# Weight transform spread over the first part and six node batches of a graph-layer kernel

## The chip, the cores and the metric

The kernel runs on one core of a Trainium2 chip. The metric is the device time of one execution in microseconds (us), lower is better. A run has several executions on the same chip as executions of the kernel before.

Names in the profile: PE is TensorE, DVE is VectorE, ACT is ScalarE, POOL is GpSimd, SP is SyncE; SPq and ACTq are the queues in which SyncE and ScalarE issue transfers. PEclk is the clock that the throttle granted to TensorE, 1.00 being full speed. TensorE's tiles: pw is a piece of the weight transform, phT, pc and px are the transpose, conv1 and the windows of the first part; ps, pm, pd, pa and pn are s, the messages, the distances, adj and A times the messages in a node batch, and py is a frequency product.

## The reference, cut to what matters

```python
h = jnp.maximum(_layernorm(x), 0.0)                    # x: 32 batches, 512 x 256, f32
xc = transpose(h)
c = relu(bn1(conv1d(xc, conv1_w, 0)))                  # conv1: 1 tap
c = bn2(conv1d(c, conv2_w, 8))                         # conv2: 17 taps
x_conv = transpose(relu(c + xc))
s = h @ w_se.T + b_se
A = exp(-distance(s)) * adj                            # 512 x 512 a batch
x_nmp = A @ relu(h @ w_msg.T + b_msg)
return x + GRU(concat(x_conv, x_nmp), h)
```

The kernel computes conv2 in a frequency domain. For that the 17-tap weights are transformed once, in 16 pieces ("the weight transform"), and written to a DRAM tensor WD. The 32 batches go in two groups of 16. For group 0 the order is: first part (layer norm, transpose, conv1, windows to frequency), then node batches (A, the messages, x_nmp), then the same first part for group 1, then the rest. Forty frequency products a group use the transformed weights, and each product needs all 16 pieces.

## The kernel before

```python
def load_taps(gen, pc):                                 # 8 transfers
    t = W2P[pc] = gen.tile([P, PI, D], FP, tag="w2p", bufs=2)
    for q in range(4):
        # ... two nc.sync.dma_start into rows of t ...

def weights_to_freq(gen, pc, part):                     # one piece
    for q in range(4):
        WST[q] = gen.tile([ROWS, SI, D], FP, tag="wst", bufs=6)     # staging
    # ... 8 matmuls pw, each into a PSUM bank ...
            for q in range(4):
                if q % 2:
                    nc.vector.tensor_copy(dst, src)     # eviction to staging
                else:
                    nc.scalar.copy(dst, src)
    for q in range(4):
        nc.sync.dma_start(WD[:, i0 : i0 + SI, :], WST[q])

def load_x(b):
    X[b] = work.tile([P, NC, D], FP, tag="x", bufs=2)
    nc.sync.dma_start(X[b], x[b].rearrange("(c p) d -> p c d", p=P))

# layer_norm(b):   statistics on VectorE, rstd on GpSimd, normalising on VectorE
# transpose_h(b):  phT on TensorE, hT = relu(phT) on VectorE, hT to DRAM (HD) on SyncE's queue
# conv1(b):        pc on TensorE, h = pc + shift on VectorE, relu on ScalarE
# windows_to_freq: px on TensorE, xf on ScalarE

def first_part(g, xf, between):
    # ...
    for b in range(b0, b1):
        if b + 1 < b1:
            layer_norm(b + 1)
        if b + 2 < b1:
            load_x(b + 2)
        between(b - b0)
        conv1(b)
        if b + 1 < b1:
            transpose_h(b + 1)
        windows_to_freq(b, xf)

with phase("first", "gen"):
    load_taps(gen, 0); load_taps(gen, 1)
    early = 12
    def between(i):
        for pc, part in spread(pieces, i, early) if i < early else []:
            weights_to_freq(gen, pc, part)
            if part == PI // SI - 1 and pc + 2 < QI // PI:
                load_taps(gen, pc + 2)
        # ...
    first_part(0, xf, between)
with phase("pw"):
    with phase("nodes"):
        # load_nodes, embed, message of batch 0
        for b in range(GB):
            mine = spread(units, b, GB)                 # 40 products over 16 batches
            affinity(b); load_nodes(b + 1)              # hT and adj of the next batch
            # ... products, embed(b + 1), aggregate(b), message(b + 1), save ...
    with phase("first"):
        first_part(1, xf, lambda i: None)               # group 1
    # ...
```

A scheduler fixes the order of each engine's instructions at build time, and the transfers that an engine issues stand in that same order.

## Time and profile before

| kernel before | |
|---|---|
| median of 3 runs | 2271.43 us (2270.57 to 2273.3) |
| end of group 0's first part (last px) | 249.4 us |
| node stage of group 0 (from there to group 1's first phT) | 378.4 us |
| group 1's first part begins | 627.8 us |

I use three marks: the end of the last px of group 0, the first phT of group 1, and the difference, which I call the node stage. The next line is the table of busy times of the kernel before for that node stage. Columns: stretch, its length, then busy us of PE, weight loads, DVE, ACT and POOL with counts, then the granted clock, the DMA share and GB/s.

```profile
249.40:627.80 378.40, 378.40 (x1437) 247.28 (x1436) 104.77 (x167) 123.95 (x201) 28.28 (x39) 1.00 0.62 213
```

TensorE is busy for the whole 378.40 us at clock 1.00.

### The profile page before, as it was taken

Reading aid. Unit: us, or ns where it says so; the run is one execution under the profiler, and the core shown is the slowest. Engines: PE = TensorE matmul, PEld = TensorE weight load, DVE = VectorE, ACT = ScalarE, POOL = GpSimd, SP = SyncE. Lnnn points to the kernel's source line nnn. Section 1 sums busy time; section 2 is a strip of 40 time slices with the busy share of each in tenths; the row PEclk is TensorE's granted clock in tenths of the full one; section 3 lists DMA queues with packets and bytes.
Section 4 is the critical chain, followed back from the end, with each engine's and each line's share of the span. In section 5 each row is a group of like instructions: output and inputs, shape, how many; then the busy total and the mean of one; then the engine's idle time right before and its main releaser. Section 6 shows DMA issues by size and latency. Waiting matters only on the chain.

```text
span 2270.3 us, 20711 instructions
## 1 busy us (share of the span) xinstructions
PE 2197.3 (97%) x8000; PEld 1316.4 (58%) x8000; DVE 744.6 (33%) x1416; ACT 596.5 (26%) x946; POOL 93.0 (4%) x119
## 2 busy tenths in 40 slices
PE   5888999999999999999999999999999999999998
PEld 4556666666688555555555554555555555555554
DVE  5556422223277122321321222223322222222323
ACT  1333333333234211111111111322222322222221
POOL 1000100000011000000000000000000000000000
PEclk7888999999999999999999999999999999999999
DMA  7878665665554453464464443222222222222210
GB/s 207 275 228 264 202 235 197 221 217 198 199 190 153 119 181 118 148 194 126 129 187 132 147 143 81 71 75 64 73 64 76 78 73 64 64 64 64 64 37 19
DMA packets 207650, 308.89 MB, mean 136 GB/s; under 512 B 11713, under 2 KB 158145, under 8 KB 207553
## 3 DMA queue, kind: packets, MB, share of 16 engines
q1 hardware_dynamic: 193152, 272.93, 39.2%
q10 hardware_dynamic: 14401, 34.65, 4.1%
q8 instruction: 63, 1.03, 0.2%
q14 instruction: 34, 0.28, 0.0%
HBM read 202.68 MB, written 104.86 MB: 135 GB/s over the span
## 4 chain that ended last, share of the span: by engine, by line
PE 91%; DVE 4%; DMA 3%; issue 1%; POOL 1%; ACT 0%; SPq 0%; DVEq 0%; POOLq 0%; ACTq 0%
PE pg L411 29%; PE pgi L411 10%; PE pn L371 10%; PE py L309 9%; PE pc L401 5%; PE pd L357 5%; PE pgh L411 5%; PE pm L345 5%; PE pc L266 4%; PE pa L362 2%; PE ps L329 2%; PE px L280 2%; PE pw L216 1%; PE po L453 1%; DMA x<-in_x_dram 1%; DVE stats L235 1%
## 5 line engine op out<-in xcount | busy, mean ns | idle before, releaser
L411 PE MATMUL pg<-nmp,wih 128*128 128x512 f32 x512 | 240.8, 592 | 0.0
L411 PE MATMUL pg<-hT,whh 128*128 128x512 f32 x512 | 240.6, 592 | 0.0
L411 PE MATMUL pg<-xconv,wih 128*128 128x512 f32 x512 | 240.6, 592 | 0.0
L426 ACT ACTIVATE rz<-pg,brz 128x512 f32<-128x512 f32 x128 | 87.9, 687 | 555.3 <-PE pg L411 549.8
L371 PE MATMUL pn<-A,msg 128*128 128x512 f32 x512 | 224.9, 592 | 0.0
L363 DVE TENSOR_TENSOR A<-e,pa 128x512 f32<-128x512 f32 x128 | 86.6, 687 | 396.6 <-ACT e L359 395.6
L314 DVE COPY y<-py 128x256 f32<-128x256 f32 x78 | 33.1, 425 | 416.4 <-PE py L309 407.8
L411 PEld LDWEIGHTS pg<-xconv,wih 128*128 128x128 f32 x512 | 97.3, 190 | 122.5 <-issue 122.5
L411 PEld LDWEIGHTS pg<-nmp,wih 128*128 128x128 f32 x512 | 97.2, 190 | 122.0 <-issue 121.7
L371 PEld LDWEIGHTS pn<-A,msg 128*128 128x128 f32 x512 | 97.2, 190 | 122.0 <-issue 114.0
L411 PEld LDWEIGHTS pg<-hT,whh 128*128 128x128 f32 x512 | 97.0, 190 | 108.6 <-issue 104.3
L309 PE MATMUL py<-wt,xf 128*128 128x256 f32 x640 | 152.7, 381 | 0.0
L438 ACT ACTIVATE n<-n,vec 128x512 f32<-128x512 f32 x64 | 46.2, 722 | 329.3 <-DVE n L437 329.3
L401 PEld LDWEIGHTS pc<-back,yt 120*128 120x128 f32 x1024 | 121.9, 195 | 18.4 <-issue 18.3
L309 PEld LDWEIGHTS py<-wt,xf 128*128 128x128 f32 x640 | 121.8, 191 | 16.4
L266 PE MATMUL pc<-w,hT 128*128 128x256 f32 x512 | 130.7, 413 | 0.4 <-DVE hT L254 0.4
L357 PE MATMUL pd<-sr,sl 96*128 96x512 f32 x256 | 131.1, 593 | 0.0
L401 PE MATMUL pc<-back,yt 120*128 120x80 f32 (+1 forms) x1024 | 120.6, 277 | 3.2 <-DMA yt<-yd 3.2
L266 PEld LDWEIGHTS pc<-w,hT 128*128 128x128 f32 x512 | 105.0, 209 | 29.0 <-ACT wst L225 12.2
L411 PE MATMUL pgh<-hT,whh 128*128 128x512 f32 x256 | 120.3, 592 | 0.0
L411 PE MATMUL pgi<-nmp,wih 128*128 128x512 f32 x256 | 120.3, 592 | 0.0
L411 PE MATMUL pgi<-xconv,wih 128*128 128x512 f32 x256 | 120.3, 592 | 0.0
(78 smaller groups left out, 2364.7 us busy)
## 6 DMA issues: line engine op xcount, KB each, us to landing
wt<-wd SPq DMA_DIRECT2D x160, 384.0 KB
x<-in_x_dram SPq DMA_DIRECT2D x64, 512.0 KB
adj<-in_adj_dram SPq DMA_DIRECT2D x32, 1024.0 KB
wd<-wst SPq DMA_DIRECT2D x64, 480.0 KB
yd<-y ACTq DMA_DIRECT2D x80, 384.0 KB
yt<-yd SPq DMA_DIRECT2D x64, 480.0 KB
hT<-hd SPq DMA_DIRECT2D x48, 512.0 KB
hd<-hT SPq DMA_DIRECT2D x32, 512.0 KB
```

The source lines that it names most:

```text
L266: nc.tensor.matmul(p[:, j, :], HT[b][:, ic, c * P : (c + 1) * P], w1[:, ic, :], start=(ic == 0), stop=(ic == DC - 1))
L280: nc.tensor.matmul(p[:, j * 2 * L : (j + 1) * 2 * L], H1[b][:, c0 + j, ic * P : (ic + 1) * P], fwd, start=True, stop=True)
L309: nc.tensor.matmul(dst, v[:, ic, :], wt[:, ic, k, :], start=(ic == 0), stop=(ic == DC - 1))
L329: nc.tensor.matmul(p[:96, :], wse[:, ic, :], HT[b][:, ic, :], start=(ic == 0), stop=(ic == DC - 1))
L345: nc.tensor.matmul(p[:, j, :], HT[b][:, ic, c * P : (c + 1) * P], wmsg[:, ic, :], start=(ic == 0), stop=(ic == DC - 1))
L357: nc.tensor.matmul(pd, SL[b % 2][:, m], SR[b % 2], start=True, stop=True)
L363: nc.vector.tensor_mul(A[b][:, mc, :], e, pa)
L371: nc.tensor.matmul(p, MSG[b][:, mc, dc * P : (dc + 1) * P], A[b][:, mc, :], start=(mc == 0), stop=(mc == NC - 1))
L401: nc.tensor.matmul(p[:, t0:t1], YT[b][w][:, oc * P : (oc + 1) * P], back[:, u0 : u0 + t1 - t0], start=(w == 0), stop=(w == W - 1), skip_gr ...
L411: nc.tensor.matmul(p, w, v, start=(i == 0), stop=(i == len(terms) - 1))
L426: nc.scalar.activation(RZ[b][:, g, :], p, AF.Sigmoid, bias=brz[:, g : g + 1], scale=1.0)
L438: nc.scalar.activation(n, n, AF.Tanh, bias=b_in[:, i : i + 1], scale=1.0)
```

## The change

The intent: the 16 pieces no longer all stand in the first part, which they slow, but 7 there and 9 in node batches 0 to 5, where TensorE is at full clock and the DMA engines have room. The products follow in node batches 6 to 15, four a batch. To make room for the node tiles, the staging buffers go from six to five.

```diff
@@ weights_to_freq
-            WST[q] = gen.tile([ROWS, SI, D], FP, tag="wst", ..., bufs=6)
+            WST[q] = gen.tile([ROWS, SI, D], FP, tag="wst", ..., bufs=5)
@@ main
-        with phase("first", "gen"):
-            early = 12
-            def between(i):
-                for pc, part in spread(pieces, i, early) if i < early else []:
-                    weights_to_freq(gen, pc, part)
-                    ...
-            first_part(0, xf, between)
+        EARLY, HEAD = 6, 7
+        with phase("gen"):
+            load_taps(pools["gen"], 0)
+            load_taps(pools["gen"], 1)
+            def between(i):
+                transform_pieces(spread(pieces[:HEAD], i, GB))
+                ...
+            with phase("first"):
+                first_part(0, xf, between)
+            with phase("nodes"):
+                nodes(0, EARLY, lambda b: [partial(transform_pieces, [piece])
+                                           for piece in spread(pieces[HEAD:], b, EARLY)])
         with phase("pw"):
             pw = pools["pw"]
             units = list(range(UNITS))
             with phase("nodes"):
-                load_nodes(0)
-                ...
+                nodes(EARLY, GB, lambda b: [partial(product, pw, 0, u, xf)
+                                            for u in spread(units, b - EARLY, GB - EARLY)])
```

(`nodes` is the old node loop as a function; cuts are marked by dots.)

More of the change, by code (lines that the diff above doesn't have):

```diff
@@ L1 @@
 from contextlib import ExitStack, contextmanager
+from functools import partial
 import numpy as np
@@ L209, in weights_to_freq @@
         for q in range(4):
-            WST[q] = gen.tile([ROWS, SI, D], FP, tag="wst", name=f"wst_{pc}_{part}_{q}", bufs=6)
+            WST[q] = gen.tile([ROWS, SI, D], FP, tag="wst", name=f"wst_{pc}_{part}_{q}", bufs=5)
         for s in range(0, SI, per):
@@ L497, in freq_tile, with transform_pieces, nodes @@
             return fpool.tile([P, DC, L, P], FP, tag="xf", name=f"xf_{g}")
-        with phase("first", "gen"):
-            gen = pools["gen"]
-            pieces = [(pc, part) for pc in range(QI // PI) for part in range(PI // SI)]
-            load_taps(gen, 0)
-            load_taps(gen, 1)
-            early = 12
+        xf = freq_tile(0)
+        pieces = [(pc, part) for pc in range(QI // PI) for part in range(PI // SI)]
+        def transform_pieces(mine):
+            for pc, part in mine:
+                weights_to_freq(pools["gen"], pc, part)
+                if part == PI // SI - 1 and pc + 2 < QI // PI:
+                    load_taps(pools["gen"], pc + 2)
+        def nodes(first, last, between):
+            load_nodes(first)
+            embed(first)
+            message(first)
+            for b in range(first, last):
+                todo = between(b)
+                affinity(b)
+                if b + 1 < last:
+                    load_nodes(b + 1)
+                for step in todo[:2]:
+                    step()
+                if b + 1 < last:
+                    embed(b + 1)
+                aggregate(b)
+                if b + 1 < last:
+                    message(b + 1)
+                save_nmp(b)
+                HT.pop(b)
+                for step in todo[2:]:
+                    step()
+        EARLY, HEAD = 6, 7
+        with phase("gen"):
+            load_taps(pools["gen"], 0)
+            load_taps(pools["gen"], 1)
             def between(i):
-                for pc, part in spread(pieces, i, early) if i < early else []:
-                    weights_to_freq(gen, pc, part)
-                    if part == PI // SI - 1 and pc + 2 < QI // PI:
-                        load_taps(gen, pc + 2)
+                transform_pieces(spread(pieces[:HEAD], i, GB))
                 if i == 2:
                     load_weights()
-            xf = freq_tile(0)
-            first_part(0, xf, between)
+            with phase("first"):
[3 more added lines that the diff above has]
+                                           for piece in spread(pieces[HEAD:], b, EARLY)])
         with phase("pw"):
@@ L522, in gnn_layer @@
             with phase("nodes"):
-                load_nodes(0)
-                embed(0)
-                message(0)
-                for b in range(GB):
-                    mine = spread(units, b, GB)
-                    affinity(b)
-                    if b + 1 < GB:
-                        load_nodes(b + 1)
-                    for u in mine[:2]:
-                        product(pw, 0, u, xf)
-                    if b + 1 < GB:
-                        embed(b + 1)
-                    aggregate(b)
-                    if b + 1 < GB:
-                        message(b + 1)
-                    save_nmp(b)
-                    HT.pop(b)
-                    for u in mine[2:]:
-                        product(pw, 0, u, xf)
+                nodes(EARLY, GB, lambda b: [partial(product, pw, 0, u, xf)
+                                            for u in spread(units, b - EARLY, GB - EARLY)])
             with phase("first"):
```

## The prediction

> **What bounds the kernel now.** I read the slices first, then busy times cut at the borders of the stages, then the chain of waits, then instructions in order of time. From the page:
>
> ```profile
> PE   5888999999999999999999999999999999999998
> ...
> PEclk7888999999999999999999999999999999999999
> DMA  7878665665554453464464443222222222222210
> ```
>
> and busy times by stretch (columns: stretch, its length, then busy us of PE, weight loads, DVE, ACT, POOL, then granted clock, DMA share, GB/s):
>
> ```profile
> 41.00:249.00 208.00, 175.91 (x845) 130.34 (x845) 125.08 (x326) 76.73 (x153) 16.12 (x16) 0.84 0.77 246
> 249.00:628.00 379.00, 379.00 (x1441) 247.86 (x1440) 104.77 (x167) 123.98 (x202) 28.28 (x39) 1.00 0.62 212
> 628.00:742.00 114.00, 107.19 (x628) 95.20 (x626) 84.96 (x247) 44.69 (x93) 14.12 (x14) 1.00 0.50 169
> ```
>
> The reader is to see that 2020 of 2270 us are TensorE at full clock with hardly a gap; only the first 249 us are not. They hold the first part of group 0 (16 batches: layer norm, transpose, conv1, windows to frequency) with all 16 pieces of the weight transform inside the first twelve batches. The third line is the **same first part for group 1 without any piece: 114 us**. From conv1 of batch 1 to the end it takes 744.5 - 638.2 = 106 us there and 249.4 - 46.4 = 203 us in group 0, where 14 pieces stand in that stretch: (203 - 106) / 14 = 6.9 us a piece, while the chain of waits shows what TensorE needs for a piece and for the rest of a batch:
>
> ```profile
> 80.56 0.87 PE phT L253 x8
> 81.44 0.55 PE px L280 x4
> 81.98 0.03 issue
> 82.01 1.90 PE px L280 x12
> 83.91 1.92 PE pw L216 x16
> 85.83 3.67 PE pc L266 x16
> ```
>
> A piece is 1.92 us of TensorE. Why it costs 7: each moves 4 x 480 KB to DRAM plus 0.5 MB of taps, and twelve batches take 1,1,2,1,1,2... pieces. Where there are two, the second has no free staging buffer (six buffers, four to a piece) and waits for the first one's writes:
>
> ```profile
> 99.55 3.92 PE L216 MATMUL pw<-w2p,taps 17*120 17x512 f32 x24
> ...
> 106.52 3.25 PE L216 MATMUL pw<-w2p,taps 17*120 17x512 f32 x8 [3.05 <-DVE wst L223]
> ...
> 109.71 5.11 PE L266 MATMUL pc<-w,hT 128*128 128x256 f32 x16
> ```
>
> TensorE stops for 3.05 us behind an eviction into a staging tile, and the conv1 that follows runs at a lowered clock (5.11 us against 3.45 where the clock is full). Starts of successive conv1 in the chain: 75.4, 85.8, 109.8, 124.2, 135.8, 158.7 us: 23 to 24 us for a batch with two pieces, 10.4 to 14.9 for one piece.
>
> **What the Trainium skill says.** (1) "Perfetto Trace Analysis", Optimization Strategy: kernels whose most-contended engine changes over time can gain from interleaving the regimes. That is this change; the trace agrees that there are two regimes (DMA 0.77 and TensorE at 0.84 clock, then TensorE alone). (2) "TensorE: Matmul & The Clock Gate", Part 1: the clock falls back when TensorE has been idle for a window of about 3.4 us. The trace agrees in kind: clock 0.84 in the first stage, 1.00 in the third line, whose gaps are short. (3) "DMA: Bandwidth & Descriptors", Anatomy of one DMA: a fixed 2 us or so, mostly the write receipt, then the bytes. The chain shows one staging write at 5.28 us; that is how long the next piece's buffer is gone, queue excluded. (4) Same page, Specifications: about 358 GB/s of HBM per core. In slices of 5 us the trace reaches 364 and 365 GB/s at shares of 0.95 and 0.98, so that is the ceiling here, and averages of 246 leave bursts that hit it.
>
> **The change part by part.** It adds no arithmetic. Seven pieces stay in the first part, at batches 2,4,6,9,11,13,15, never two in one batch. Nine go into node batches 0 to 5 (1,2,1,2,1,2). The 40 products of group 0 go to node batches 6 to 15, four each. TensorE's order from the first part of group 1 on is identical in both built programs, so all the change is before 628 us.
>
> *Start-up.* In the kernel before, the second x tile is issued at 30.6 us, behind the tap loads, and conv1 of batch 1 starts at 46.4 after a piece. The tap loads and their place ahead of x stay. Without the piece, conv1 of batch 1 should start near 41 us.
>
> *First part.* In the group-1 stage one batch is 1.90 + 3.45 + 0.12 + 0.70 + 0.64 = 6.9 us in the chain (px, conv1, transpose, DVE, ACT). DVE's own work there is 4 x (0.41 + 0.17 + 0.41) + 0.17 + 2 x 0.68 + 2 x 0.68 = 6.9 us, and a piece adds 4 x 0.684 = 2.7: 9.6 us. The quiet one-piece batches measured 10.4 and 10.6. I take 10.1 with a piece (full clock) and 7.2 without (the group-1 stage averages 99.2 / 14 = 7.1, late x tiles included). From conv1 of batch 1: 7 x 10.1 + 7 x 7.2 + 7 for the last = 128 us. End of the first part: 41 + 128 = 169 us instead of 249. **Saved: 80 us.**
>
> *Node batches 0 to 5.* One batch without products is, in the chain, 1.72 (ps) + 6.87 (pn) + 3.45 (pm) + 4 x 1.30 (pd, pa) = 17.2 us of TensorE. Check: 16 x 17.2 + 40 x 2.59 (a product) = 379, the measured stage, so nothing is hidden in it. Nine pieces at 1.92 add 17.3 if none waits. **Given back: 17 us.**
>
> *Waits in them.* A pair of pieces needs 16 evictions, eight on each engine: DVE 5.5 us against 3.8 of TensorE, 1.7 lost; then the second piece wants four staging tiles of which only one is free now (five instead of six), so evictions stand some 5 us for the writes behind a 1 MB adjacency load, PSUM banks stay full, and pn starts perhaps 2.5 late. About 4.2 us a pair, three pairs 12.6; 0.7 for each single piece 2. **About 15 us.** DMA in these batches: 2.0 MB of adjacency, h and result, 1.5 x 2.5 of pieces, 5.8 MB per 20 us = 290 GB/s: below 365, above the 246 of the old stage.
>
> *Border after batch 5.* Every product reads all pieces, so its first weight tile waits for the last writes, and in the built queue the adjacency load of batch 6 stands behind that tile. Writes of the last pair end perhaps 15 us after the pieces start; then 1 MB and 0.4 MB, some 6 us. TensorE has 5 + 6.9 + 1.7 + 3.5 + 0.9 = 18 us of other work. **About 5 us lost.**
>
> *Node batches 6 to 15.* 10 x 17.2 + 40 x 2.59 = 276 us, as before per unit of work. 5.1 MB in 27.6 us is 185 GB/s; each weight tile has at least 2.6 + 5.2 + 2.6 = 10 us between release and use, so no wait.
>
> Sum: 169 + 6 x 17.2 + 17 + 15 + 5 + 276 = 585 against 628: 43 us less. 2271.4 - 43 = **2228 us**, or 1.9%.
>
> **The rivals.** *Moved, not removed:* the pairs with only five staging buffers stall node batches as they stalled the first part (two pieces cost about 10 us of TensorE time there, 99.55 to 109.77, against 3.84). Then each pair loses 6 to 8 more, with a clock penalty, the border 10 to 12, and the gain falls to 15 to 20 us: about 2253. For it: the same buffer wait, a fuller queue. Against: evictions are not DVE's bound in a node batch (105 of 379 us busy), and pn, pm have operands ready. *All hidden:* DMA has 20 us a batch and the scheduler's order puts other evictions between; pieces cost 1.92, border nothing, first part as good as the group-1 stage (9.6 and 6.9 a batch, 164 us). Then 164 + 103 + 17 + 276 = 560, gain 68: 2203. *DMA bound in the first part still:* 2 batches with one piece move 2.1 + 2.5 MB in 17.3 us = 266 GB/s, more than the old mean. If so a pair of batches takes 20 us, the first part ends near 188 (41 + 7 x 20 + 7) and the time is 2247.
>
> **Range and chances.** First part +-9, waits +-9, border +-5 make about +-14 us for one sigma: 8 in 10 from 2210 to 2247. Faster by over 2% needs under 2226, a gain of 45, a sixth of a sigma beyond my 43: 0.43. Within 2%: 0.56. Slower needs every rival at once: 0.01.
>
> **What would show it.** Right: node stage starts at 165 to 175 us, clock over 0.9 before it; pw matmuls run from about 50 to 290 us; TensorE idle 10 to 25 us in node batches 0 to 5, ended by staging evictions or their DMA; a gap of a few us before pa of batch 6 ended by an adjacency load; the last 1642 us (from the first part of group 1 on) alike. Wrong: first part past 185 us (DMA was its bound, not the pairs), pairs taking over 8 us of TensorE, or a gap over 10 us at the border; or, on the good side, no gaps at all.

## The result

| | before | after |
|---|---|---|
| median (range, runs) | 2271.0 us (2265.89 to 2273.3, 4) | 2268.93 us (2264.42 to 2270.49, 4) |
| first part of group 0 ends | 249.4 | 202.2 (predicted 169) |
| node stage of group 0 | 378.4 | 426.8 (predicted 416) |
| group 1's first part begins | 627.8 | 629.0 (predicted 585) |

The ratio of after to before is 0.9991, 95% interval 0.9968 to 1.0013: the same. Here and below, a ratio is the mean time of one kernel's runs over that of the other's of the same rounds, so it is not quite the ratio of the medians quoted. All outputs are right.

The first part got 47 us shorter and the node stage 48 us longer. The slices of the kernel after (40 equal slices of 56.7 us; tenths):

```profile
PE   4888998999999999999999999999999999999998
...
PEclk8899999999999999999999999999999999999999
DMA  5656767777654454463463442222222222222210
```

Compared with the prediction's first fence, TensorE is below 90% in the first four slices as it was, and now in the seventh too (340 to 397 us, the border after node batch 5): the unfilled time is spread, not gone. Busy times of the kernel after by stretch (columns as above):

```profile
202.15:357.00 154.85, 137.84 (x527) 76.14 (x527) 62.75 (x113) 60.94 (x104) 3.42 (x4) 0.94 0.72 234
357.00:628.96 271.96, 271.96 (x1054) 186.18 (x1055) 70.21 (x117) 81.55 (x133) 26.85 (x37) 0.99 0.69 243
628.96:742.00 113.04, 106.91 (x629) 95.32 (x627) 85.49 (x247) 45.17 (x93) 14.11 (x14) 1.00 0.50 179
```

The first line holds node batches 0 to 5. It has 154.85 - 137.84 = 17.0 us in which TensorE stands still, and clock 0.94. The second, node batches 6 to 15, has no idle time, and the third, group 1's first part, is as it was before. TensorE's instructions of the kernel after that stood still longest, in order of time (start, length, the group of instructions, in brackets the idle time before it and what ended it):

```profile
39.00 2.19 PE L254 MATMUL phT<-ident,x 128*128 128x128 f32 x8 [19.26 <-DVE x L243]
...
107.47 2.15 PE L254 MATMUL phT<-ident,x 128*128 128x128 f32 x8 [4.29 <-issue]
...
138.07 3.83 PE L281 MATMUL px<-fwd,h 128*128 128x160 f32 x16 [3.13 <-ACT h L271]
...
206.86 3.70 PE L330 MATMUL ps<-hT,wse 128*96 128x512 f32 x4 [4.71 <-DMA hT<-hd]
...
268.35 3.70 PE L330 MATMUL ps<-hT,wse 128*96 128x512 f32 x4 [3.75 <-DMA hT<-hd]
...
296.22 7.13 PE L372 MATMUL pn<-A,msg 128*128 128x512 f32 x16 [0.93 <-DVE wst L224]
...
357.00 1.09 PE L363 MATMUL pa<-ident,adj 128*128 128x128 f32 x4 [7.63 <-DMA adj<-in_adj_dram]
```

The first line is the start-up: TensorE waits 19 us for the layer norm of the second batch. Then there are stops of 3 to 4 us in batches of the first part, and four stops in the node stage: 4.71 + 3.75 + 0.93 + 7.63 = 17.0 us, all of the idle time there. The three large ones end on a transfer (hT, hT, adj). What follows a stop is slow: ps takes 3.70 us after them against 1.88 us undisturbed. TensorE's busy time in the node stage is 137.84 + 271.96 = 409.8 us against 378.4 + 17.3 for nine pieces, so 14.1 us more come from such lengthened instructions. Together 31 us of waits and lengthened instructions, on top of the pieces' own 17.3.

SyncE's queue in the first part shows how late an x tile can be issued (start, length of the issue, line, transfer):

```profile
131.16 7.38 SPq L229 DMA_DIRECT2D wd<-wst  x4
138.63 1.28 SPq L205 DMA_DIRECT2D w2p<-in_w2T_dram  x1
...
145.20 0.45 SPq L94 DMA_DIRECT2D x<-in_x_dram  x1
```

The piece's four writes and the next eight tap loads take the queue from 131.16 to 144.6 us. The x tile behind them is issued at 145.20, although TensorE had finished with its buffer (the phT at 133.90) at 134.9 us. VectorE's order costs time as well: between 127 and 136.7 us it finishes one layer norm, runs the next and copies four evictions before it comes to the hidden layer's add, and px waits (the line at 138.07 us in the fence before). Which of the two holds a batch these lines don't say. At the two stops of 4.29 us VectorE reached the layer norm only behind the hidden layer's add (the later one: add until 154.99, normalising from 158.04, phT at 158.56 us), and no wait for x is recorded there.

### The profile page after: what moved, and what is told of

It reads as the page before. It is cut to its first block, busy times and chain, and to the rows that moved or that the text cites. A ratio compares the mean times of both kernels' runs of the same rounds, so it can differ in the third digit from the quotient of the medians.

```text
span 2268.7 us, 20734 instructions
## 1 busy us (share of the span) xinstructions
PE 2178.8 (96%) x8000; PEld 1306.9 (58%) x8000; DVE 744.1 (33%) x1416; ACT 595.9 (26%) x946; POOL 92.9 (4%) x119
## 4 chain that ended last, share of the span: by engine, by line
PE 91%; DMA 3%; DVE 3%; ACT 1%; issue 1%; SPq 0%; POOL 0%; ACTq 0%; DVEq 0%; POOLq 0%
PE pg L412 29%; PE pn L372 10%; PE pgi L412 10%; PE py L310 9%; PE pc L402 5%; PE pgh L412 5%; PE pd L358 5%; PE pm L346 5%; PE pc L267 4%; PE px L281 3%; PE ps L330 2%; PE pa L363 2%; PE pw L217 1%; PE po L454 1%; DMA x<-in_x_dram 1%; DVE h L270 1%
## 5 line engine op out<-in xcount | busy, mean ns | idle before, releaser
L372 PE MATMUL pn<-A,msg 128*128 128x512 f32 x512 | 226.3, 595 | 0.9 <-DVE wst L224 0.9
L267 PE MATMUL pc<-w,hT 128*128 128x256 f32 x512 | 121.2, 391 | 0.6 <-DVE hT L255 0.6
L346 PE MATMUL pm<-wmsg,hT 128*128 128x256 f32 x512 | 117.0, 382 | 0.0
```

The source lines that it names most:

```text
L267: nc.tensor.matmul(p[:, j, :], HT[b][:, ic, c * P : (c + 1) * P], w1[:, ic, :], start=(ic == 0), stop=(ic == DC - 1))
L346: nc.tensor.matmul(p[:, j, :], HT[b][:, ic, c * P : (c + 1) * P], wmsg[:, ic, :], start=(ic == 0), stop=(ic == DC - 1))
L372: nc.tensor.matmul(p, MSG[b][:, mc, dc * P : (dc + 1) * P], A[b][:, mc, :], start=(mc == 0), stop=(mc == NC - 1))
```

## The experiments

Eighteen runs, all with three rounds. The edits are against the kernel after unless said otherwise. By the record's threshold of 2% only e21 counts as faster and all others as the same; smaller differences are read from the ratios and their intervals.

| run | time, median us | ratio to before | first part ends | node stage |
|---|---|---|---|---|
| before | 2271.0 | 1 | 249.4 | 378.4 |
| after | 2268.9 | 0.9991 | 202.2 | 426.8 |
| e6_before_even | 2274.4 | 1.0014 | 250.6 | 379.6 |
| e1_x_own_queue | 2275.3 | 1.0025 | 195.7 | 424.8 |
| e2_evict_on_act | 2261.8 | 0.9964 | 195.6 | 425.7 |
| e4_extra_traffic | 2302.4 | 1.0133 | 221.2 | 431.7 |
| e10_queue_and_act | 2280.9 | 1.0035 | 209.3 | 428.3 |
| e11_queue_act_three | 2277.4 | 1.0019 | 204.5 | 427.3 |
| e7_node_queue | 2264.2 | 0.9960 | 197.7 | 419.6 |
| e12_all | 2274.9 | 1.0015 | 207.8 | 421.6 |
| e3_x_three | 2259.9 | 0.9943 | 190.1 | 424.3 |
| e13_three_act | 2258.1 | 0.9930 | 184.9 | 428.6 |
| e14_three_act_wq | 2309.3 | 1.0160 | 226.3 | 439.9 |
| e15_all_scalar_queue | 2300.5 | 1.0122 | 219.6 | 436.3 |
| e16_norm_on_gpsimd | 2260.5 | 0.9946 | 190.8 | 427.7 |
| e17_node_side_too | 2235.7 | 0.9848 | 179.1 | 414.1 |
| e18_before_same_repairs | 2245.4 | 0.9889 | 222.1 | 378.4 |
| e19_all_three | 2245.3 | 0.9891 | 189.4 | 415.1 |
| e20_nodes_only | 2258.8 | 0.9937 | 203.8 | 408.7 |
| e21_x_first | 2221.7 | 0.9774 | 164.5 | 414.7 |

The 95% intervals are within 0.0033 of each ratio. Medians of the kernel before in these jobs lie between 2269.0 and 2274.1 us.

### Were pairs of pieces the cause? (e6)

```diff
 # the kernel before
-            early = 12
+            early = 16
```

> The kernel before, with its sixteen pieces one to each of the sixteen batches instead of 1,1,2,1,1,2 over twelve. The prediction's reading (pairs of pieces are what costs 7 us a piece; a single piece costs a batch 10.1 to 10.4): conv1 of batch 1 at 46, then 15 batches of 10.4, node stage from about 205, time 2227. If single pieces stall as well (queue order): batches of 13 or more, node stage from 240 or later, time within 10 us of the kernel before.

Every batch has exactly one piece now and none has two. The last px and the first ps (timeline of TensorE in this run):

```profile
247.00 3.57 PE L280 MATMUL px<-fwd,h 128*128 128x160 f32 x12 [2.20 <-ACT h L270]
250.36 3.11 PE L329 MATMUL ps<-hT,wse 128*96 128x512 f32 x4
```

The first part ends at 250.6 us, as before. The prediction's reading, that a piece costs 6.9 us because the second of a pair finds no staging buffer, falls: single pieces cost the same. From conv1 of batch 1, at 44.5 us in this run, a batch with one piece takes (250.6 - 44.5) / 15 = 13.7 us, not 10.1.

### One suspected cause at a time (e1, e2, e4)

```diff
 # e1: x tiles 1 to 15 issued by GpSimd
-        nc.sync.dma_start(X[b], ...)
+        q = nc.gpsimd if 0 < b < GB and b not in seen else nc.sync
+        q.dma_start(X[b], ...)
 # e2: all evictions on ScalarE
-                if q % 2:
-                    nc.vector.tensor_copy(dst, src)
-                else:
-                    nc.scalar.copy(dst, src)
+                nc.scalar.copy(dst, src)
 # e4: half of each first-part piece written twice more, from ScalarE's queue
+            if q % 2 == 0 and (PI // SI) * pc + part < 7:
+                for k in range(2):
+                    scr = dram.tile([ROWS, SI, D], FP, ...)
+                    nc.scalar.dma_start(scr, WST[q])
```

> The changed kernel, but the x tiles 1 to 15 of group 0's first part are loaded from GpSimd's DMA queue instead of SyncE's. Theory Q (x loads stand behind staging writes and tap loads in one in-order queue, so the layer norm comes late): besides the start-up gain (x tile 1 no longer behind the tap loads, conv1 of batch 1 near 25 instead of 43.6 us) the batches after it fall from a mean of 10.8 to about 8.7 us, so the node stage starts near 155-160 instead of 207 us and the time falls by 40 us or more. Theory D (the evictions of a piece on DVE) and theory B (DMA bandwidth): only the start-up, 15 to 20 us; batches stay at 10.5 or more.

> The changed kernel, but all evictions of the weight transform are on ACT (none on DVE). Theory D: DVE loses 2.7 us a piece, the 14 batches from conv1 of batch 1 on shorten by about 7 x 2.7 = 19 us, time 2250. Theory Q: the x tiles are as late as before; under 8 us. Theory B: nothing.

> The changed kernel, with two of the four staging tiles of each of the first part's seven pieces written twice more to scratch memory from ACT's queue: 1.97 MB more a piece, 13.8 MB in all, result unchanged. Theory B: the first part is bound by bytes, so it lengthens by 13.8 MB at about 0.35 MB/us = 39 us. Theories Q and D: the bytes fit into gaps (DMA share 0.55 to 0.66 there), under 10 us.

Neither the queue nor the evictions alone did what was expected of them, and e4 fell between its two forecasts (39 us and under 10). With e1 conv1 of batch 1 started at 33 us in place of 43.6, but from then on px waited 3 to 4 us on the hidden layer four times, and the first part gained 6.5 us only. With e2 the evictions left VectorE, but the transposes still waited 4.3 us twice. The extra 13.8 MB of e4 cost 19 us to the end of the first part, and some 32 us in all (1.4%). The trace shows how the extra bytes reach TensorE. These are waits of e4 and then of the kernel after between 41 and 203 us (engine and line, what it waited for, us in total, times, longest):

```profile
DVE stats L240 <- DMA x<-in_x_dram: 29.3, 4, 10.8
PE phT L258 <- DVE x L247: 26.4, 2, 14.2
```

```profile
PE phT L254 <- issue: 8.6, 2, 4.3
DVE stats L236 <- DMA x<-in_x_dram: 6.4, 2, 6.2
```

The statistics wait for x tiles that land late behind the burst: 29.3 us in place of 6.4. The DMA engines are not full on average (share 0.67 to 221 us); it is the lateness of one tile that counts. A part of e4's cost may be the issues in ScalarE's order instead: the waits of px rose from 16.3 to 22.2 us.

### Two repairs that did not add up (e10, e11), and the node queue (e7, e12)

```diff
 # e10: e1 and e2.  e11: e10, a third x buffer, loads three tiles ahead.
 # e7: hT (node batches 0 to 6) and adj (0 to 5) loads on GpSimd's queue, adj of batch 6 on ScalarE's;
 #     the products' pool made larger (wt 4, both 3 buffers in group 0) and reopened after the nodes,
 #     so that the second pool of node tiles should not lie on staging tiles
-        nc.sync.dma_start(ADJ[b], ...)
+        (nc.gpsimd if b < EARLY else nc.scalar if b == EARLY else nc.sync).dma_start(ADJ[b], ...)
-        nc.sync.dma_start(HT[b], HD[b])
+        (nc.gpsimd if first_use else nc.sync).dma_start(HT[b], HD[b])
 # e12: e11 and e7.
```

> The change plus both repairs of the first part at once: x tiles 1 to 15 of the first group on GpSimd's queue, and all evictions of the weight transform on ScalarE. Theory A (two causes in series: the x tile that is issued late behind the bursts, and the four evictions that stand before the hidden layer's add in VectorE's order; each alone gains little because the other takes its place): the first node batch starts at about 165 us or before (206.9 with the change, 199.8 and 200.6 with one repair each), and the time is 2235 us or less. Theory B (the bytes that a piece moves set the pace of a batch with a piece, whatever queue or engine): it starts at 190 us or later, and the time stays at 2255 us or more.

> As the run before, with a third x buffer and the loads three tiles ahead. If with both repairs the x tile is still late because its transfer shares the wires with a piece's writes (theory B in part), the third buffer hides that: first node batch 10 us or more earlier than without it. If issue order and VectorE were all (theory A), it starts within 4 us of the run without it, and the time is the same within 6 us.

> The first part is left as the change has it; in the node stage of the first group the loads of hT and adj no longer stand in SyncE's queue behind the pieces' bursts, and staging buffers do not hold them. If the 30 us of waits that the node stage gained come from that order, the gaps at the first node batch (4.7 us), at the next hT (3.75) and at the sixth border (7.6), with the cold clock after them, shrink: node stage 410 to 415 us in place of 426.8, and 2255 us or so. If the bytes of the pieces cause them, the node stage stays at 422 us or more, and the time is the same within 6 us.

> All repairs together: first part by GpSimd's queue, ScalarE and three x buffers, node stage by the other queues. If gains add (theory A, with the node stage's own cause), first part ends at 155 to 165 us, node stage 410 to 418 us, and the time is 2205 to 2220 us. If what the first part gains is given back in the node stage, because the weights or hT are not there yet, the node stage is 430 us or longer and the time is 2235 us or more.

Together e1 and e2 are slower than each alone: 209 us against 196. My theory A expected 165. The table of transfers points to a reason; it is the line for x tiles of e1, then of e10, between 41 and 203 us (size, median us from issue to landing):

```profile
x<-in_x_dram POOLq DMA_DIRECT2D x11, 512.0 KB, 4.6
```

```profile
x<-in_x_dram POOLq DMA_DIRECT2D x11, 512.0 KB, 7.6
```

With ScalarE evicting alone the four writes of a piece leave within 3.8 us, where in e1 most took 7 to 10, and the next x tile runs beside the whole burst: 7.6 us to landing against 4.6 (in e10 an x tile is issued at 72.34 us, in the middle of a burst that leaves from 69.25 to 73.0, and the next statistics wait 9.2 us, until 82.87). The statistics wait 49.6 us for x in e10, in eight waits of up to 9.6 us. A third buffer gave only 4.7 us here (e11); the x tiles stay late, with waits up to 10.2 us, and in GpSimd's order a load that waits for its buffer stands between the rstd computations; I take this to be the reason, but did not test it by itself. The reading that a faster eviction moved the burst onto the transfer that mattered fits these lines; nothing else about GpSimd's queue was separated from it.

e7 left the first part alone. The gaps at the second hT and at the border shrank (the latter to 1.4 us) but the first ps now waited 10 us for an hT tile from GpSimd's queue. The node stage gained 7 us, not the 12 to 17 expected: part of its waits comes from what stands before hT and adj, or from the pool memory that e7 changed with it. e12 adds nothing to e11's first part and took 2274.9 us where I had expected 2205 to 2220.

### Depth in place of another queue (e3, e13, e16)

```diff
 # e3: SyncE's queue stays; a third x buffer in the first part of group 0, loads three tiles ahead
+        if b < GB and b % 3 == 2 and b not in seen:
+            X[b] = pools["first"].tile([P, NC, D], FP, tag="x3", bufs=1)
@@ first_part
+        if g == 0:
+            load_x(b0 + 2)
-            if b + 2 < b1:
-                load_x(b + 2)
+            if g == 0 and b + 3 < b1:
+                load_x(b + 3)
+            elif g and b + 2 < b1:
+                load_x(b + 2)
 # e13: e3 and all evictions on ScalarE
 # e16: e13 and, in the first part of group 0, the normalising of layer norm on GpSimd
-            nc.vector.tensor_scalar(XN[b][:, c, :], ...)
+            (nc.gpsimd if b < GB else nc.vector).tensor_scalar(XN[b][:, c, :], ...)
```

> The change with a third x buffer and the x loads three tiles ahead, still on SyncE's queue. Theory D (depth: an x tile that is issued or lands up to 10 us late behind a piece's burst holds the layer norm only because two buffers give it no slack): the waits of VectorE's statistics on x and of the transposes on the layer norm vanish between 60 and 200 us, and the first part ends at 190 us or before (202.2 with the change). Rival (the order of VectorE, with the piece's evictions and the next layer norm ahead of the hidden layer's add, is what holds): it ends at 196 us or later.

> The third buffer and, besides, all evictions of the transform on ScalarE. With GpSimd's queue the two repairs did not add: an x tile took 7.6 us from issue to landing there, and its issue stood before the rstd in GpSimd's order. If that alone spoiled the sum, they add here: first part ends at 175 us or before and the time is 2245 us or less. If the bytes of a piece beside x and hd set the pace of the pairs of batches, it ends at 188 us or later and the time is 2258 us or more.

> Three x buffers, ScalarE evictions, and the normalising of the first group's first part on GpSimd, so that VectorE neither does it nor waits 1.2 us for the rstd. If VectorE's order holds the rest of the first part, the waits of px on the hidden layer (19 us in the run without) fall below 8 us and the first part ends at 176 us or before (184.9 without). If GpSimd is too slow at it (over 8 us for a tile), the transposes wait for it instead and the first part ends later than 190 us.

The third buffer by itself gave 12 us in the first part (202.2 to 190.1) and about 0.5% of the time against the kernel after (0.9943 and 0.9991 of before). This is what the Trainium skill's "Perfetto Trace Analysis" (Optimization Strategy) describes: the same gap repeating on the engine that should be full can mean too few buffers. The gaps of 4.3 us before phT, two of them in the kernel after, are gone. The waits for x that the trace records hardly changed (5.6 us, 6.4 before): what the timelines show instead is that a layer norm is finished one batch ahead, so that phT (148.08 us in e3) no longer follows a layer norm that stands behind the add. ScalarE's evictions gave 5 us more in the first part of which 2 us arrived in the time. e13's expectation of 175 us was missed; the longest wait that remains stands in VectorE's order. VectorE, then TensorE, in e13, around a batch with a piece:

```profile
119.15 1.39 DVE L246 TENSOR_SCALAR x<-x,mv,rstd 128x256 f32<-128x256 f32 x4 [1.19 <-POOL rstd L243]
120.45 0.75 DVE L239 BATCH_NORM_STATS2 stats<-x 128x6 f32<-128x256 f32 x2
...
123.58 1.38 DVE L246 TENSOR_SCALAR x<-x,mv,rstd 128x256 f32<-128x256 f32 x4 [1.19 <-POOL rstd L243]
124.88 1.28 DVE L273 TENSOR_TENSOR h<-pc,shift_row 128x512 f32<-128x512 f32 x2
```

```profile
114.94 3.72 PE L270 MATMUL pc<-w,hT 128*128 128x256 f32 x16
...
126.28 4.10 PE L284 MATMUL px<-fwd,h 128*128 128x160 f32 x14 [6.75 <-ACT h L274]
```

conv1 (pc) was done at 118.7 us. VectorE first finishes one layer norm, runs the next, waits 1.2 us for GpSimd's rstd in each, and comes to the hidden layer's add (h) at 124.88. px waits 6.75 us. I had feared that the piece's evictions stand in that order; with those gone the layer norms stand there.

e16 takes the normalising out of that order. The waits of px fell from 19.0 to 8.9 us, close to the theory's 8, but the transposes then waited for GpSimd (8.3 us beyond the start-up), which takes 4.8 us for a tile against 1.4 on VectorE, and the first part ended at 190.8, later than without. So the waits of px do come from what stands in VectorE's order, and this cure is none.

### Another queue again: ScalarE's (e14, e15)

```diff
 # e14: e13, with the pieces' writes and the later taps issued by ScalarE
-            nc.sync.dma_start(WD[:, i0 : i0 + SI, :], WST[q])
+            nc.scalar.dma_start(WD[:, i0 : i0 + SI, :], WST[q])
+            eng = nc.scalar if pc >= 2 else nc.sync
+            eng.dma_start(t[...], src[...])              # taps
 # e15: e14, the second x tile issued before the first taps, the products' pool as in e7
```

> As the run before, and the pieces' writes and later taps issued from ScalarE's queue, so that nothing of the transform stands before x, hT or adj in SyncE's queue. If issue order still counts with three buffers, the first part ends 5 us or more earlier than in the run before and the node stage of the first group shrinks from 426 to 415 us. If only the wires count, both stay within 3 us, or grow because ScalarE's issues (0.9 us each) delay the hidden layer's relu.

> As the run before, with the second x tile issued ahead of the first taps (the start-up wait of 19 us of TensorE shrinks to 10) and the product pool's memory kept apart from what the pieces use, so that the load of adj at the sixth border need not wait. If these add: first part 8 us shorter than in the run before, border wait 7.6 to under 2 us, and the time is 12 us or more below it, 2240 us or less. If what is gained in the first part is taken back by waits in the node stage, the time is within 6 us of it.

This was a clear loss, 1.6% and 1.2%. ScalarE in e14 (ACTq are its transfer issues):

```profile
81.94 1.58 ACTq L212 DMA_DIRECT2D w2p<-in_w2T_dram  x1
...
90.67 0.63 ACTq L213 DMA_DIRECT2D w2p<-in_w2T_dram  x1
91.34 1.15 ACT L275 ACTIVATE h<-h 128x512 f32<-128x512 f32 x2 [11.55 <-DMA w2p<-in_w2T_dram]
```

Eight tap loads hold ScalarE from 81.94 to 91.3 us, and the hidden layer's relu stands behind them: 11.55 us here, and 10.4 to 11.6 us three times in the first part. SyncE's queue, full as it is, has no arithmetic in it. Moving a burst to an engine that computes moves the wait onto the chain.

### The node side as well (e17, e18, e19)

```diff
 # e17: e13 and
-                transform_pieces(spread(pieces[:HEAD], i, GB))
+                transform_pieces(spread(pieces[:HEAD], i, GB - 2))   # none in the last two batches
 #      hT of node batches 2 to 6 and adj of 0 to 5 on GpSimd's queue, adj of 6 on ScalarE's,
 #      the products' pool as in e7
 # e18: the kernel BEFORE with e13's repairs (third x buffer, evictions on ScalarE)
 # e19: e17 and e16's normalising on GpSimd
```

> Three x buffers and ScalarE evictions (2258 us, node stage of the first group 423 to 428 us from the last px), and on the node side: no piece in the last two batches of the first part, later hT and adj loads on GpSimd's queue, memory of the products kept apart from the pieces. If the node stage's waits come from bursts that stand before hT and adj, the gaps at the first batch (5.3 us) and at the border (4.8 us) and the cold clock after them go, and the node stage takes 410 us or less: 2245 us. If they come from the bytes, it stays at 420 us.

> The kernel before, with a third x buffer and all evictions on ScalarE, all 16 pieces still in the first part. If the repairs act on the layer norm's chain whatever the spread, its first part ends at 225 us or before (249.4) and the time is 2247 us or less, so that the spread gains nothing against it (2258 us). If the pieces' own bytes and evictions bound it, it ends at 240 us or later, and the time is 2262 us or more.

> All of e16 and e17. If both add: first part 170 to 178 us, node stage 400 to 412 us, 2225 to 2240 us. If one takes back what the other gives, 2250 us or more.

e17 is faster than both kernels: 2235.7 us, 0.9848 (0.9828 to 0.9867). Its first part is also 5.8 us shorter than e13's, with its seven pieces over fourteen batches. Busy times of its node stage, and the first instructions of TensorE in it:

```profile
179.08:330.00 150.92, 149.00 (x559) 81.16 (x557) 41.70 (x72) 80.71 (x144) 11.50 (x16) 0.95 0.70 233
330.00:593.22 263.22, 262.88 (x1024) 179.97 (x1024) 67.13 (x112) 79.08 (x129) 26.18 (x36) 1.00 0.70 245
```

```profile
178.92 1.88 PE L337 MATMUL ps<-hT,wse 128*96 128x512 f32 x4
...
186.26 0.63 PE L370 MATMUL pa<-ident,adj 128*128 128x128 f32 x4 [1.15 <-DMA adj<-in_adj_dram]
```

The gap before the first ps is gone, since no piece's burst stands before the hT load any more. TensorE's idle time in the stage is 2.3 us in place of 17.0. The stage still takes 414 us, not the 396 of pure addition (410 or less was expected). The trace puts most of the difference at the three pairs of pieces. One of them in e17, then one in e20 (below), where VectorE still takes half of the evictions:

```profile
255.07 6.36 PE L223 MATMUL pw<-w2p,taps 17*120 17x512 f32 x32
261.37 3.58 PE L337 MATMUL ps<-hT,wse 128*96 128x512 f32 x4
```

```profile
234.52 4.85 PE L217 MATMUL pw<-w2p,taps 17*120 17x512 f32 x32
239.30 1.96 PE L334 MATMUL ps<-hT,wse 128*96 128x512 f32 x4
```

With ScalarE alone evicting, TensorE goes at ScalarE's pace (its weight loads for pw wait 5.8 us for ScalarE's evictions in the stage), the granted clock is 0.85 from 210.22 to 219.64 us around the first pair, and what follows a pair is slow: ps 3.4 and 3.6 us, and pn 10.02 us in place of 7.03 after the third. From start to start the nine pieces take 25.6 us in e17 (17.3 was their own), and the instructions after the pairs 6 us more: with the idle time some 17 of the 18 us. So the eviction that helped the first part (5.2 us from e3 to e13) costs the node stage about as much (4.3 us from e3 to e13); mixed evictions in the node batches with ScalarE's in the first part were not tried.

e18 is the sober control. The same two repairs in the kernel before, all 16 pieces in its first part, give 2245.4 us: its first part shrinks by 27 us and its node stage stays at 378.4. This is better than the change with those repairs (e13, 2258.1). So the repairs do not need the spreading, and the spreading pays only once the node side is repaired too: e17 is 9.7 us faster than e18 by the medians of the same job. e19 shows again that normalising on GpSimd costs: 10 us more than e17.

### The node side alone, and the start (e20, e21)

```diff
 # e20: after, with the node side of e17 only (two x buffers, mixed evictions)
 # e21: e17, and
             with phase("first"):                # these loads move here; their old places go
+                load_x(1)
+                load_x(2)
+                load_taps(pools["gen"], 0)
+                load_taps(pools["gen"], 1)
                 first_part(0, xf, between)
```

> The change with the node side alone: no piece in the last two batches of the first part, hT and adj of the early node batches on GpSimd's queue, product memory kept apart; two x buffers and mixed evictions as in the change. If the gains of both sides are separate: node stage 414 us as in the run with all (426.8 with the change), first part 195 to 202 us, 2252 to 2258 us. If the node side gains only together with ScalarE's evictions (whose absence delays the pieces), the node stage is 420 us or more: 2262 us.

> Run e17 with the second and third x tiles issued ahead of the taps. If the 20.9 us wait before the second batch is a cost, its transposes start at about 20 us in place of 39.2, the first part ends at 162 to 172 us (179.1) and the time is 2219 to 2228 us (2235.7). If the taps, now late, hold the first piece or the memory system slows all of it, the first part ends at 176 us or later and the time is the same within 6 us.

e20 takes 18 us out of the node stage (426.8 to 408.7) and is 0.63% faster than before. Its node stage is 5 us shorter than e17's, which differs by the third x buffer and by all evictions on ScalarE (the fences of the pairs above show where). e20 changes placement, queues and memory at once, so their shares are not separated.

e21 moves two x loads ahead of 16 tap loads and gives 14 us more by the medians of two jobs: 2221.7 us, 0.9774 (0.9758 to 0.979), the best kernel, 2.3% faster than before and as the first forecast had it. The same start in the kernel before with e18's repairs was not tried, so how much of the 2.3% is the spreading's own is not shown; by e17 and e18 it is about 10 us. TensorE's second phT starts at 19.46 us in place of 39.2, conv1 of batch 1 at 26.80 in place of 43.6 in the kernel after, and the first part ends at 164.5:

```profile
19.46 1.04 PE L257 MATMUL phT<-ident,x 128*128 128x128 f32 x8
...
26.80 3.72 PE L270 MATMUL pc<-w,hT 128*128 128x256 f32 x16
```

```profile
DVE stats L239 <- DMA x<-in_x_dram: 0.9, 2, 0.7
```

The waits for x (second fence) are 0.9 us; they were 5.9 in e17 and 6.4 in the kernel after. The prediction had taken the start-up as given ("The tap loads and their place ahead of x stay"), and it was one of the largest single costs of the first part.

## Why the prediction was wrong

It said 2228 us with a range from 2210 to 2247; 2268.9 came. By its own steps:

- **What bounds the kernel: right.** The part from group 1 on is alike (1640 us after, 1642 before), and all the change lies before it.
- **Start-up: right in size.** conv1 of batch 1 was put at "near 41 us" and came at 43.6.
- **First part: the step that failed.** "I take 10.1 with a piece (full clock) and 7.2 without", ending at 169 us. It ended at 202.2. From the starts of conv1, the interval that holds a piece's matmuls is 8.8 us in four of seven cases and 10.7 on average, but the interval after it, put at 7.2, is 11.0 on average (up to 14.2). Only the one interval without a neighbour took 6.8. The sum, with unrounded intervals, is 158.5 us against the 128 of the prediction. The 10.1 rested on a sum of VectorE's busy times (9.6) and two quiet batches (10.4 and 10.6), and the 7.2 on the stage without pieces; neither asked what a piece does to the batch after it. The traces show a chain instead (x issued and landed, layer norm, transpose, and the hidden layer's add behind whatever VectorE has before it), which a piece disturbs for a batch longer than it lasts. With the 2.6 us of the start-up this is 33 of the 44 us by which group 1 began later than predicted.
- **The cause given for a piece's 6.9 us: wrong.** "the second has no free staging buffer": without any pair the first part took the same time (e6).
- **The rival that DMA bounds the first part:** its sign was right and its form was not. More bytes cost time (e4), yet in e18 the same first part moves 286 GB/s in place of 246 after the repairs. A third x buffer took 12 us away with the same bytes (e3). The prediction's reading that 365 GB/s is the ceiling here was wrong too: in e18 the slices of 5 us from 35 and 40 us moved 401 and 394 GB/s.
- **Node batches, the pieces' own time: right.** Nine pieces at 1.92 us, 17.3 us. **Waits: too small and in other places.** The prediction had 12.6 us in pairs, 2 in single pieces and 5 at the border, 20 in all, and 31 came. The pairs cost 1.0 us each beyond their own 3.84 (4.85 in all where the clock was full), not 4.2. The border cost 7.6 and about 3 of slow clock, not 5. Not foreseen were the first ps (4.7 us), an hT load behind eight writes and eight tap loads (3.75 us), and the slow clock after each. In e7, e17 and e20 most of these waits shrink when hT and adj no longer stand behind the pieces' transfers; the pool memory was changed with it each time.
- **The clock, its point (2):** the trace agrees in kind only with what it took from the Trainium skill's "TensorE: Matmul & The Clock Gate" (Part 1). In the kernel before, conv1 took 6.44 us after a recorded stop of 1.07 us at 121.83, with the clock at 1.00 before it, far less than a window of 3.4; and the clock fell in e17 at pairs without a recorded stop. Point (3) takes its 2 us from a section on transfers that GpSimd issues, while the staging writes are SyncE's; the 5.28 us measured is the number to use.
- **Node batches 6 to 15: right.** 272 us from the border on; 276 was predicted with some 6 us of batch 6 that lie before the border.
- **Its own alarm** ("first part past 185 us") named the right observation with the DMA-bound reading; the runs put order and depth in its place. That the time came out within 0.1% of before is a coincidence of two sums, 47 us gained and 48 lost. Where the expected gain went: 47 us were gained in the first part; 17 of that were given back as the pieces' own TensorE time, and 31 as new waits and lengthened instructions.

Open stay the shares of e17's node edits, the shares of late x tiles and of VectorE's order in the first part, a cure for that order, and the spreading's own worth in the best kernel.

## What to carry to other kernels

In this kernel the stage whose engines were all below full was a chain. In such a stage add up the path of one tile through each engine's order and each transfer's queue, not the busy times, and look at the unit after the disturbed one as well. Before work is moved out of such a stage, try one more buffer for the tile that comes late and the order of the first loads; here these gave 24 us in the kernel that kept the work in place (e18, buffer and evictions) and 14 more in the changed one (e21, first loads). A burst moved to another engine's queue, or evicted faster, lands on something else: check what stands behind it and what shares its moment.

## What the Trainium skill lacked or had wrong

- "DMA: Bandwidth & Descriptors", Issuing engines are not separate DMA queues: it says that spreading issues over engines only saves sequencer time, usually small relative to the DMA. It lacks the price on the other side. In e14 eight tap loads held ScalarE for 9.4 us and its relu waited 11.55 us behind them; the kernel lost 1.6%. And the issue time adds up in a burst: eight tap loads (four of 128 KB, four of 8 KB) took SyncE's queue for 6.0 us in the kernel after, from 138.63.
- "DMA: Bandwidth & Descriptors", Latency and other measured facts: it gives first-byte figures of some 1 us for transfers issued by GpSimd. For planning under load it lacks a figure from issue to landing; here 512 KB issued by GpSimd took 4.6 us in e1 and 7.6 us in e10, the two runs differing in the evictions, and with them in how closely a burst of writes ran beside it.
- "GPSIMD Engine Reference", Engine selection: it calls elementwise operations with one input roughly line-rate on GpSimd, and puts those with two inputs at about half of VectorE's speed. Normalising 128 x 256 f32 (one tensor and two per-partition scalars) took 1.22 us on GpSimd in e16, while VectorE does four of them in 1.38 us in e13: a factor of 3.5 at this size.
